# V1 and V0 as 32 by 64 matmuls over row groups, with their operand loaded by DMA, and the bias constant's matmuls in a later step

## The chip, the cores and the metric

The kernel runs on one core of one Trainium2 chip. Time is device time in microseconds of that core, the median of several executions. The engines are named as the profile names them: PE is TensorE (PEld its weight loads), DVE is VectorE, ACT is ScalarE, POOL is GpSimd, and SP is SyncE, which only issues DMAs here. Each engine runs its own instructions in program order and waits on semaphores for the others.

## The reference

A compressed interaction network (CIN) over x of shape (1024, 64, 16): batch, F = 64 features, E = 16. Three layers; the first two keep half of their outputs as the next h, and only sums over E of the outputs reach the result, through one row of weights.

```python
for i in range(3):
    z = jnp.einsum('bfe,bge->bfge', x0, h).reshape(Bn, f0 * fh, e)
    y = jnp.einsum('oc,bce->boe', Ws[i], z) + bs[i][None, :, None]
    if i != 2:
        x_i, h = y[:, :64, :], y[:, 64:, :]
    else:
        x_i, h = y, y
    xs.append(x_i)
pooled = jnp.sum(jnp.concatenate(xs, axis=1), axis=2)
return pooled @ fc_w.T + fc_b
```

All arithmetic is in f32.

## The kernel before, in words

Because the result is one number for each batch row, the kernel never forms the outputs that only get summed. It folds the final weights into the layers: the last layer becomes a 64-column matrix Q (called w_all[:, :, 64:128]), the summed halves of layers 1 and 0 become the 64 by 64 matrices V1 (v1w) and V0 (held twice on the diagonal of bd). For each column (b, e) the result is then a sum over h1 times (Q's matmul plus V1 x), and x times (V0 x plus a constant cx).

The batch is cut into NCH = 32 chunks of 32 rows, so a chunk is N = 512 columns. A chunk's data comes in two layouts from HBM: `xa` (128 rows, 4 shifted copies, 1 MB) and `xb` (the same size), by `load_xa` and `load_xb` on SP's queue. DVE multiplies them in `product` (L212), four products j of 128 by 2048; ACT writes squares into 32 rows of the last one (L217). PE contracts the 16 tiles of a chunk with `w_all` in `contract` (L249), sixteen f32 matmuls of 128 by 128 by 512. The profile records each f32 matmul twice, as two passes.

The diagonal that the products leave out, V1 and V0 are done for four chunks at once in `contract_shared`, called with the first of them; the text calls one such call a group, and there are eight. It has three parts. L263 multiplies V1, 64 by 64, with x of a chunk: even chunks have x in rows 0 to 63 of `xxs[k]` (k = chunk // 2), odd ones in rows 64 to 127; the result goes to the other half of the chunk's accumulator. L267 multiplies V0 with the same x into `ys[k]`. L273 multiplies the squares of x (`sqs`, four chunks on four row groups of 32) with `w_sq`, as 32 by 64 tiles, eight for a group. Before the change `last_tile` makes these operands on ACT, a chunk at a time: `squares` (L223, 32 rows) and a copy into `xxs` (L232, 64 rows).

The order of work is written out by hand; no planner moves instructions. The head chunks [2, 3, 0, 1] are computed first for h1 alone, in `half_contract` (L285), while the weights Q are made from W2 and W1 (L409, L433, a round trip through DRAM `md`, and L534). PE's first work is a row of matmuls on zeros (L105), then the shift matmuls (L182) that make the second operand of the first products on chip. Early on PE also computes the bias constant `cst` (L366: fc times biases, four records, read by ACT at L370 and used at L613 when results are finished). The head's chunks 0 and 1 get their Q part at once (`head_q`, L303), chunks 2 and 3 after chunk 7.

The main loop goes over `order` = [4, 5, 6, 7, 2, 3, 8, 9, ...]. In step s it emits the loads and products of the chunk two places on (`load_products`), the contraction of chunk order[s], the group where chunk % 4 is 1 (for chunks 0 to 3, in the step of chunk 3), and `factors`, `x_v0x` and `sums` of finished chunks: ACT copies half of an accumulator (q, L319), DVE multiplies it by the other half (uu, L325), multiplies x by V0 x (L330) and sums over e (L334). V1 and V0 are made on DVE on the way, by `weigh` (L571, L572) and four copies each (L583 after chunk 4's products, L595 after chunk 5's).

Buffers set when transfers start: `xa` and `xb` have three each, products twelve (three chunks), accumulators four banks. SP issues in order, so a load that waits for a buffer holds up what is behind it.

Of the kernel before, what the change touches and what calls it, by code (L numbers as in the profile page):

```python
# [33 lines left out]
F32 = mybir.dt.float32  # L37
AF = mybir.ActivationFunctionType
# [3 lines left out]
F = 64  # L42
E = 16
B = 1024
CB = 32
N = CB * E
# [5 lines left out]
XR = 128 + NI  # L52
EXT = 96
HEAD = [2, 3, 0, 1]
NF = len(HEAD)
KEPT = HEAD[-2:]
NV = 200
FIRST = 4
# [4 lines left out]
def cin_kernel(ctx, tc, xra, xrb, wh, w0r, w1h, w2t, wx1, wx0, vec, out):  # L63
    nc = tc.nc
# [10 lines left out]
    def const_tile(name, shape):  # L75
        return const.tile(shape, F32, tag=name, name=name)
# [18 lines left out]
    fv2 = const_tile("fv2", [128, 32])  # L95
    nc.scalar.copy(fv2, fc2.to_broadcast([128, 32]))

    bd = const_tile("bd", [128, 128])

    misc = ps.tile([128, N], F32, tag="acc", name="misc", bufs=4)  # L100


    zeros = nc.const_aps.tensor(0.0, [128, 128])
    for n in (128,) * 7 + (64,):
        nc.tensor.matmul(misc[:, 0:n], zeros, zeros[:, 0:n], start=True, stop=True)  # L105

    shift = const_tile("shift", [128, 96])
# [13 lines left out]

    w_all = const_tile("w_all", [128, NT, 192])
    w_sq = const_tile("w_sq", [128, 192])
    v1w = const_tile("v1w", [128, F])


    xas, xbs, xxs, sqs = {}, {}, {}, {}

    def load_xa(c, at=slice(0, NI)):
        if c not in xas or at.start == 0:  # L130
# [9 lines left out]
    def load_xb(c, first=NJ):  # L140

        xb = xp.tile([128, NJ, N], F32, tag="xb", name=f"xb_{c}")
        for at in (slice(0, first), slice(first, NJ)):
            if at.start < NJ:
                nc.sync.dma_start(out=xb[:, at, :], in_=xrb[c, :, at, :])
        xbs[c] = [xb[:, j, :] for j in range(NJ)]

    def load_chunk(c):
        load_xa(c)
# [2 lines left out]
    c0, c1, c2, c3 = HEAD  # L152
# [63 lines left out]
        if j == NJ - 1:  # L216
            nc.scalar.activation(zs[c, j][SQ, 0, :], xas[c][SQ, 0, :], AF.Square)  # L217

    def squares(c):
        if c // 4 not in sqs:  # L220
            sqs[c // 4] = xp.tile([128, N], F32, tag="zl", name=f"sq_{c}", bufs=3)
        at = slice(32 * (c % 4), 32 * (c % 4) + 32)
        nc.scalar.activation(sqs[c // 4][at], xas[c][0:32, 0, :], AF.Square)  # L223

    def last_tile(c):

        if c >= FIRST:
            squares(c)
        if c % 2 == 0:
            xxs[c // 2] = sp.tile([128, N], F32, tag="xx", name=f"xx_{c}", bufs=5)  # L230
        to = halves[c % 2]
        nc.scalar.copy(xxs[c // 2][to], xas[c][to, 0, :])  # L232

    def w_cols(c):
        return slice(64, 192) if c % 2 else slice(0, 128)

    def tiles(j):

        return (1, 2, 3, 0) if j == NJ - 1 else range(NI)
# [14 lines left out]
    def contract_shared(first):  # L254

        chunks = range(first, first + 4)
        ends = chunks if first == 0 else chunks[:2]
        for k in (first // 2, first // 2 + 1):
            ys[k] = ps.tile([128, N], F32, tag="y", name=f"y_{k}")
            for n in range(2):  # L260
                c, rows, q = 2 * k + n, halves[n], halves[1 - n]
                for acc_c, cols in pieces(c):
                    nc.tensor.matmul(  # L263
                        acc_c[q], v1w[rows], xxs[k][rows, cols], start=(c not in ends), stop=False,
                    )
            for rows in halves:
                nc.tensor.matmul(ys[k][rows], bd[rows, rows], xxs[k][rows], start=True, stop=True)  # L267
        for c in chunks:
            at = slice(32 * (c % 4), 32 * (c % 4) + 32)
            for acc_c, cols in pieces(c):  # L270
                for n in range(2):
                    h = n == c % 2
                    nc.tensor.matmul(  # L273
                        acc_c[halves[n]], w_sq[at, w_cols(c)][:, 64 * n : 64 * n + 64],
                        sqs[first // 4][at, cols], start=h and (first == 0 or c not in ends),
                        stop=(c in ends), tile_position=(at.start, 64 * n),
                    )


    def half_contract(c, *js, last=None, at=None):  # L280
        for j in js:
            for i in at or tiles(j):
                t = j * NI + i
                for n in range(2):
                    nc.tensor.matmul(  # L285
                        accs[c][halves[n]], w_all[:, t, 0:64],
                        zs[c, j][:, i, n * H2 : (n + 1) * H2],
                        start=(t == 0), stop=(j == last and i == tiles(j)[-1]),
                    )
# [56 lines left out]


    new_acc(c0, H2)
    squares(c0)
    nc.scalar.copy(xb_gps[:, 0, :], xbs[c0][1])  # L350
    xbs[c0][1] = xb_gps[:, 0, :]
    for i in (0, 2):
# [6 lines left out]
    nc.scalar.copy(w0o[0], w0s[0][:, :, 1, :])  # L359
    h1_weights(0, w0o[0])  # L360
    product(c0, 0, 2, NI)
    half_contract(c0, 0, at=(0, 1))

    cst = const_tile("cst", [128, 1])
    for j in range(2):
        nc.tensor.matmul(  # L366
            misc[:, 0:1], fcol[:, j : j + 1].to_broadcast([128, 128]), bcol[:, j : j + 1],
            start=(j == 0), stop=(j == 1),
        )
    nc.scalar.activation(cst, misc[:, 0:1], AF.Identity, bias=fcb, scale=float(E))  # L370
    nc.scalar.copy(w0o[1], w0s[1][:, :, 1, :])
    product(c0, 2, 0, 2)
    h1_weights(1, w0o[1])
# [3 lines left out]
    nc.vector.memset(w0o[3][SQ, 0, :], 0.0)  # L377
    for j in (2, 3):
        h1_weights(j, w0o[j])
    half_contract(c0, 0, at=(2, 3))  # L380


    for j, tag in ((0, "y"), (3, "acc"), (1, "y"), (2, "set")):
# [4 lines left out]
    new_acc(c1, H2)  # L388
    nc.scalar.copy(xb_gps[:, 1, :], xbs[c1][3])
    xbs[c1][3] = xb_gps[:, 1, :]  # L390
    squares(c1)

    product(c0, 3)
    load_chunk(c3)
# [7 lines left out]


    v2r = flat_tile("v2r")[:, 0:1024].rearrange("p (n c) -> p n c", n=2)
    v2t = const_tile("v2t", [128, F])
    for n in range(2):
        pv = ps.tile([128, 512], F32, tag=("set", "y")[n], name=f"pv2_{n}")
        for k in range(4):
# [68 lines left out]
    keep_h1(c1)  # L477


    squares(c2)  # L480
    new_acc(c2, H2)
    for j in range(NJ):
        product(c2, j)
# [34 lines left out]
    new_acc(c3, H2)  # L518
    for j in range(NJ - 1):
        product(c3, j)  # L520
    squares(c3)
    keep_h1(c2)
    half_contract(c3, 0, 3, 1, 2, last=2)

    for j in range(1, NJ):
        for half in range(2):
            read_columns(j, nc.scalar if half and j == 2 else nc.sync, half)
    dg = const_tile("dg", [128, F])
    nc.sync.dma_start(out=dg[SQ], in_=m_ap(32, 32, [[row + F, 32], [1, F]]))
    nc.sync.dma_start(out=w_sq[:, 64:128], in_=m_ap(0, 0, [[0, 4], [row + F, 32], [1, F]]))  # L530

# [2 lines left out]
        nc.vector.tensor_tensor(w_all[:, at, 64:128], ms[:, 0, at], ms[:, 1, at], ALU.add)  # L534

    keep_h1(c3)
    for c in KEPT:
        last_tile(c)


    for j in range(NJ):
# [10 lines left out]
    for j in range(NJ):  # L552
        head_q(0, j)

    made = set()

    def load_products(c, other=None):

        for n in (c,) if other is None else (c, other):
            if n not in made:  # L560
                load_chunk(n)
                last_tile(n)
                made.add(n)
        for j in range(NJ):
            product(c, j)

    def weigh(w, fc, out):
# [3 lines left out]
        nc.vector.tensor_tensor(w, w, fc.unsqueeze(1).to_broadcast([128, nk, n]), ALU.mult)  # L571
        nc.vector.tensor_reduce(out, w, AX.X, ALU.add)  # L572

    load_products(FIRST)


    w1x = set_tile("w1x")
    nc.sync.dma_start(out=w1x, in_=wx1)
    v1h = const_tile("v1h", [128, 32])
    weigh(w1x, fcr[:, 64:128], v1h)  # L580
    for to in halves:
        for n in range(2):
            nc.vector.tensor_copy(v1w[to, 32 * n : 32 * n + 32], v1h[halves[n]])  # L583

    load_products(FIRST + 1)

    def v0_weights():
        w0x = flat_tile("w0x")
        nc.sync.dma_start(out=w0x, in_=wx0)
        v0h = const_tile("v0h", [128, 32])  # L590
        weigh(w0x, fcr[:, 0:64], v0h)
        for to in halves:
            for n in range(2):
                cols = slice(to.start + 32 * n, to.start + 32 * n + 32)
                nc.vector.tensor_copy(bd[to, cols], v0h[halves[n]])  # L595


    NP = NCH // 2
    QP = NP // 4
    res = const_tile("res", [128, QP, CB])  # L600
    outs = out.rearrange("(k h b) o -> h k (b o)", h=2, b=CB)

    def pool(k0, k1, part=0, **flags):
# [16 lines left out]
    for s, c in enumerate(order):  # L620
        k, head = c // 2, c in HEAD
        if order[s - 1] in HEAD and not head:
            for n in range(NF // 2):
                x_v0x(n)
            for n in HEAD:
                factors(n)
                if n % 2:
                    sums(n // 2)
        if 0 < s < len(order) - 2 and s not in (2, 3):
            load_products(*order[s + 2 : s + (4 if s == 6 else 3)])  # L630
        if s in (2, 3):

            if s == 2:
                for n in order[4:6]:
                    load_chunk(n)
                    last_tile(n)
            for j in (0, 1) if s == 2 else (2, 3):
                for n in order[4:6]:
                    product(n, j)
        if not head:  # L640
            if c % 4 < 2:
                new_acc(c)
            for j in range(NJ):
                contract(c, j)
        elif c % 2:
            for n in (c - 1, c):
                new_acc(n)
            for j in range(NJ):
                head_q(k, j)
            contract_shared(0)  # L650
        if c % 4 == 1 and not head:
            for n in (1, 2):
                new_acc(c + n)
            contract_shared(c - 1)
        if s == 0:
            v0_weights()
            load_products(order[2], order[3])

        if c == HEAD[0] or c % 4 in (0, 3) and s and order[s - 1] not in HEAD:
            factors(order[s - 1])  # L660
            if order[s - 1] % 2:
                sums(order[s - 1] // 2)
        elif c % 4 == 2 and not head:
            factors(c - 2)
            factors(c - 1)
            x_v0x(k - 1)
            x_v0x(k)
            sums(k - 1)
# [94 lines left out]
```

## Time and profile before

| | us |
|---|---|
| median of 6 runs | 486.85 |
| lowest and highest | 486.42, 487.24 |
| profiled execution | 486.5 |
| its span (first to last instruction) | 484.7 |
| PE busy | 479.1 |
| DVE busy | 370.3 |
| ACT busy | 94.4 |
| a group of L263, L267 and L273 (83.92 to 86.84) | 2.92 |
| granted TensorE clock, mean | 0.998 |
| DMA, mean over the span | 162 GB/s |

Lines of the profile name the line of the kernel, the engine, the operation, its tiles as out<-in and their shapes. "busy" is the union of the instructions' times, so parallel matmuls count once. The chain of work that ended last follows the end of the program back through whatever released each step; a line of it is start, length, engine, tile, line and number of records. A timeline line is start, length, engine, line, operation and number of records merged in it.

### The profile page before, as it was taken

The numbers are of one execution on the slowest core, as the hardware profiler recorded it, in microseconds if no ns is written. First come the engines' busy times: TensorE is split into PE (matmuls) and PEld (weight loads), VectorE is DVE, ScalarE is ACT, GpSimd is POOL, SyncE is SP. The second block draws the span as 40 slices with busy tenths as digits, with TensorE's granted clock in tenths as the row PEclk, the third lists the DMA queues.
The fourth block names the chain that finished last, engine by engine and source line by source line (L and its number), as shares of the span: only waits on it lengthen the run. The fifth ranks groups of instructions, "written<-read, shape, count | busy, mean of one in ns | idle before, by whom it ended". The sixth has DMA issues, their size and how long they took to land.

```text
span 484.7 us, 4065 instructions
## 1 busy us (share of the span) xinstructions
PE 479.1 (99%) x1674; PEld 215.6 (44%) x1674; DVE 370.3 (76%) x235; ACT 94.4 (19%) x166; POOL 15.2 (3%) x15
## 2 busy tenths in 40 slices
PE   8999999999999999999999999999999999999996
PEld 5565344443344344444444344443444434444465
DVE  5993699999899989898887686767878676771312
ACT  4254012021213030322221012212022121020001
POOL 5330000000000000000000000000000000000000
PEclk9999999999999999999999999999999999999999
DMA  8985984441743453546253344432244430000000
GB/s 340 412 259 165 423 370 174 172 174 42 319 171 163 173 191 156 185 172 272 106 216 124 141 174 173 162 133 107 118 173 173 174 144 29 1 0 0 1 1 0
DMA packets 14392, 78.59 MB, mean 162 GB/s; under 512 B 3778, under 2 KB 4450, under 8 KB 5478
## 3 DMA queue, kind: packets, MB, share of 16 engines
q1 hardware_dynamic: 13314, 77.31, 40.9%
q10 hardware_dynamic: 1060, 1.02, 0.8%
q8 instruction: 13, 0.21, 0.2%
q14 instruction: 5, 0.04, 0.0%
HBM read 76.69 MB, written 1.64 MB: 162 GB/s over the span
## 4 chain that ended last, share of the span: by engine, by line
PE 98%; DMA 1%; DVE 0%; ACT 0%; SPq 0%; issue 0%
PE acc L249 80%; PE acc L285 6%; PE acc L303 6%; PE acc L263 3%; PE acc L273 2%; DMA w0t<-in_wh 1%; PE xp L182 0%; PE pm L433 0%; PE pv L409 0%; PE y L267 0%; SPq L132 0%; PE po L605 0%; PE misc L366 0%; DVE uu L325 0%; DVE w_all L342 0%
## 5 line engine op out<-in xcount | busy, mean ns | idle before, releaser
L249 PE MATMUL acc<-z,w_all 128*128 128x512 f32 (+1 forms) x928 | 387.3, 579 | 0.0
L212 DVE TENSOR_TENSOR z<-xa,xb 128x2048 f32<-128x2048 f32 x124 | 278.4, 2286 | 40.8 <-PE acc L249 34.1
L249 PEld LDWEIGHTS acc<-z,w_all 128*128 128x128 f32 x928 | 175.5, 190 | 211.3 <-issue 205.7
L217 ACT ACTIVATE z<-xa 32x512 f32<-32x512 f32 x34 | 21.3, 626 | 318.4 <-DVE z L212 317.1
L325 DVE SCALAR_TENSOR_TENSOR uu<-acc,vs,q 64x512 f32<-64x512 f32 (+1 forms) x29 | 21.2, 732 | 57.7 <-ACT q L319 57.5
L285 PE MATMUL acc<-z,w_all 128*64 128x256 f32 x256 | 29.0, 381 | 0.9 <-DVE w_all L342 0.9
L303 PE MATMUL acc<-z,w_all 128*64 128x512 f32 x128 | 27.9, 593 | 0.0
L319 ACT COPY q<-acc 64x512 f32<-64x512 f32 (+1 forms) x33 | 18.7, 567 | 37.4 <-PE acc L249 21.2
L212 DVE TENSOR_TENSOR z<-xa,xp 128x2048 f32<-128x2048 f32 (+2 forms) x12 | 20.4, 1748 | 5.9 <-PE xp L182 5.9
L285 PEld LDWEIGHTS acc<-z,w_all 128*64 128x64 f32 x256 | 17.9, 137 | 12.7 <-issue 2.5
L223 ACT ACTIVATE sq<-xa 32x512 f32<-32x512 f32 x32 | 20.1, 628 | 8.4 <-issue 4.1
L334 DVE TENSOR_REDUCE acc<-uu 128x64 f32<-128x1024 f32 (+3 forms) x19 | 20.3, 1072 | 0.3
L232 ACT COPY xx<-xa 64x512 f32<-64x512 f32 x32 | 19.6, 613 | 0.3
L303 PEld LDWEIGHTS acc<-z,w_all 128*64 128x64 f32 x128 | 9.1, 137 | 18.0 <-issue 17.6
L267 PE MATMUL y<-xx,bd 64*64 64x512 f32 x64 | 15.5, 603 | 0.0
L263 PE MATMUL acc<-xx,v1w 64*64 64x512 f32 (+1 forms) x66 | 15.5, 588 | 0.0
L330 DVE SCALAR_TENSOR_TENSOR uu<-y,cx,xx 128x512 f32<-128x512 f32 x16 | 11.3, 746 | 0.2
L212 POOL TENSOR_TENSOR z<-xa,xb_gps 128x1024 f32<-128x1024 f32 (+1 forms) x3 | 9.3, 3102 | 5.1 <-ACT xb_gps L350 4.4
L273 PE MATMUL acc<-sq,w_sq 32*64 32x512 f32 (+1 forms) x132 | 8.9, 599 | 0.0
L263 PEld LDWEIGHTS acc<-xx,v1w 64*64 64x64 f32 x66 | 4.1, 132 | 10.6 <-issue 10.5
L534 DVE TENSOR_TENSOR w_all<-ms 128x256 f32<-128x256 f32 x4 | 1.5, 422 | 6.0 <-DMA ms<-md 6.0
L212 POOL TENSOR_TENSOR z<-xa,xb 128x2048 f32<-128x2048 f32 x1 | 4.6, 4567 | 12.9 <-DMA xb<-in_xrb 12.9
(57 smaller groups left out, 63.6 us busy)
## 6 DMA issues: line engine op xcount, KB each, us to landing
xa<-in_xra SPq DMA_DIRECT2D x32, 1024.0 KB, 4.8
xb<-in_xrb SPq DMA_DIRECT2D x31, 1024.0 KB, 6.9
w<-in_w2t SPq DMA_DIRECT2D x2, 1024.0 KB, 10.9
xa<-in_xra SPq DMA_DIRECT2D x2, 768.0 KB, 7.9
w1s<-in_w1h SPq DMA_DIRECT2D x1, 1024.0 KB
w1x<-in_wx SPq DMA_DIRECT2D x1, 1024.0 KB
w0x<-in_wx SPq DMA_DIRECT2D x1, 1024.0 KB, 9.1
w0t<-in_w0r SPq DMA_DIRECT2D x1, 768.0 KB
```

What stands on the lines that cost most here:

```text
L212: engine.tensor_tensor(zs[c, j][:, at, :], xas[c][:, at, :], xbs[c][j].unsqueeze(1).to_broadcast([128, last - first, N]), ALU.mult,)
L217: nc.scalar.activation(zs[c, j][SQ, 0, :], xas[c][SQ, 0, :], AF.Square)
L223: nc.scalar.activation(sqs[c // 4][at], xas[c][0:32, 0, :], AF.Square)
L232: nc.scalar.copy(xxs[c // 2][to], xas[c][to, 0, :])
L249: nc.tensor.matmul(acc_c, w_all[:, t, w_cols(c)], zs[c, j][:, i, cols], start=(t == 0 and c % 4 < 2), stop=(t == NT - NI and c % 4 >= 2),)
L263: nc.tensor.matmul(acc_c[q], v1w[rows], xxs[k][rows, cols], start=(c not in ends), stop=False,)
L273: nc.tensor.matmul(acc_c[halves[n]], w_sq[at, w_cols(c)][:, 64 * n : 64 * n + 64], sqs[first // 4][at, cols], start=h and (first == 0 or c ...
L285: nc.tensor.matmul(accs[c][halves[n]], w_all[:, t, 0:64], zs[c, j][:, i, n * H2 : (n + 1) * H2], start=(t == 0), stop=(j == last and i == ...
L303: nc.tensor.matmul(accs[c][halves[1 - c % 2]], w_all[:, t, 64:128], zs[c, j][:, i, :], start=(t == 0), stop=False,)
L319: nc.scalar.copy(q[h, cols], acc_c[64 - h.start : 128 - h.start])
L325: nc.vector.scalar_tensor_tensor(uu[:, cols], acc_c[h], bh1[h], q[h, cols], ALU.add, ALU.mult)
L334: nc.vector.tensor_reduce(acc[rows, of, k, half], uus[k][rows, of, E * half.start : E * half.stop].rearrange("p k (b e) -> p k b e", e=E), ...
```

## The change

Four things change.

- `load_shared(first)` takes the place of `squares` and `last_tile`. For the four chunks of a group it loads `xr`, a tile of 128 rows by 2 by 512, by one DMA for each chunk: row group n (32 rows) holds chunk first + n, features 0 to 31 in part 0 and 32 to 63 in part 1. Another DMA for each chunk loads `xxs`, which DVE still reads in `x_v0x`. One ACT instruction squares part 0 for all four chunks. It is called where the chunk 4k+1 is loaded, and for chunks 0 to 3 in step 2.
- In `contract_shared` V1 and V0 become 32 by 64 matmuls, two (m = 0, 1) for each chunk and matrix, accumulated over the two halves of the features. The tile positions put chunk c on rows 32 (c % 4) and the two matrices on the two column halves. Weights are `v1w` and `v0w`, each on all four row groups, filled by `to_groups`, 16 ACT copies of 32 by 32 each, in place of the DVE copies.
- The bias constant's matmuls move from the start to step 9 (before the contraction of chunk 11), with a PSUM tile of their own. The contraction of chunk 2's first product, which they split in two, is emitted in one piece.
- One zero matmul of 128 columns fewer at the start (seven in place of eight), and some tiles share storage (v2t, dg and res; shift, v1h and v0h).

```diff
-    for n in (128,) * 7 + (64,):
+    for n in (128,) * 6 + (64,):
         nc.tensor.matmul(misc[:, 0:n], zeros, zeros[:, 0:n], start=True, stop=True)
...
+    def load_shared(first):
+
+        xr = xrs[first] = sp.tile([128, 2, N], F32, tag="xr", name=f"xr_{first}")
+        for k in (first // 2, first // 2 + 1):
+            xxs[k] = sp.tile([128, N], F32, tag="xx", name=f"xx_{k}", bufs=4)
+        for n in range(4):
+            c = first + n
+            nc.sync.dma_start(
+                out=xr[32 * n : 32 * n + 32],
+                in_=bass.AP(
+                    tensor=xra.tensor, offset=c * XR * N, ap=[[N, 32], [32 * N, 2], [1, N]]
+                ),
+            )
+            nc.sync.dma_start(out=xxs[c // 2][halves[c % 2]], in_=xra[c, 0:F])
+        sqs[first] = sp.tile([128, N], F32, tag="sq", name=f"sq_{first}")
+        nc.scalar.activation(sqs[first], xr[:, 0, :], AF.Square)
...
-            for n in range(2):
-                c, rows, q = 2 * k + n, halves[n], halves[1 - n]
+        groups = {c: slice(32 * (c % 4), 32 * (c % 4) + 32) for c in chunks}
+        for m in range(2):
+            for c, at in groups.items():
+                n, xr = c % 2, xrs[first][groups[c], m]
                 for acc_c, cols in pieces(c):
                     nc.tensor.matmul(
-                        acc_c[q], v1w[rows], xxs[k][rows, cols], start=(c not in ends), stop=False,
+                        acc_c[halves[1 - n]], v1w[at, m], xr[:, cols],
+                        start=(m == 0 and c not in ends), stop=False,
+                        tile_position=(at.start, 64 * (1 - n)),
                     )
-            for rows in halves:
-                nc.tensor.matmul(ys[k][rows], bd[rows, rows], xxs[k][rows], start=True, stop=True)
+                nc.tensor.matmul(
+                    ys[c // 2][halves[n]], v0w[at, m], xr, start=(m == 0), stop=(m == 1),
+                    tile_position=(at.start, 64 * n),
+                )
...
-    half_contract(c0, 0, at=(0, 1))
-
-    cst = const_tile("cst", [128, 1])
-    for j in range(2):
-        nc.tensor.matmul(
-            misc[:, 0:1], fcol[:, j : j + 1].to_broadcast([128, 128]), bcol[:, j : j + 1],
-            start=(j == 0), stop=(j == 1),
-        )
-    nc.scalar.activation(cst, misc[:, 0:1], AF.Identity, bias=fcb, scale=float(E))
...
-    half_contract(c0, 0, at=(2, 3))
+    half_contract(c0, 0)
...
-                last_tile(n)
+                if n % 4 == 1:
+                    load_shared(n - 1)
...
+    def to_groups(w, part):
+
+        for at in range(0, 128, 32):
+            for n in range(2):
+                for m in range(2):
+                    q = 64 * n + 32 * m
+                    nc.scalar.copy(
+                        w[at : at + 32, m, 32 * n : 32 * n + 32], part[q : q + 32]
+                    )
...
-    for to in halves:
-        for n in range(2):
-            nc.vector.tensor_copy(v1w[to, 32 * n : 32 * n + 32], v1h[halves[n]])
+    to_groups(v1w, v1h)
...
-        for to in halves:
-            for n in range(2):
-                cols = slice(to.start + 32 * n, to.start + 32 * n + 32)
-                nc.vector.tensor_copy(bd[to, cols], v0h[halves[n]])
+        to_groups(v0w, v0h)
...
+        if s == len(HEAD) + 5:
+
+            pc = ps.tile([128, 1], F32, tag="set", name="pc")
+            for j in range(2):
+                nc.tensor.matmul(
+                    pc, fcol[:, j : j + 1].to_broadcast([128, 128]), bcol[:, j : j + 1],
+                    start=(j == 0), stop=(j == 1),
+                )
+            nc.scalar.activation(cst, pc, AF.Identity, bias=fcb, scale=float(E))
```

## The prediction

> **What bounds the kernel now.** I read the busy shares first, then the chain of work that ended last, then that chain in order of time, then TensorE's timeline in the stretches that the edit touches. All times are of the profiled execution: 486.5 us, of which 484.7 are span and 1.8 lie around it. The median of the six runs, 486.85, is 0.35 above it.
>
> ```profile
> PE 479.1 (99%) x1674; PEld 215.6 (44%) x1674; DVE 370.3 (76%) x235; ACT 94.4 (19%) x166; POOL 15.2 (3%) x15
> ...
> PE 98%; DMA 1%; DVE 0%; ACT 0%; SPq 0%; issue 0%
> ```
>
> PE is busy for 99% of the span and carries 98% of the chain; DVE, at 76%, is next and has room. So only what shortens or stalls PE's stream counts. The chain in order of time, around a group of shared matmuls:
>
> ```profile
> 7.63 1.08 PE acc L285 x8
> 8.71 0.54 PE misc L366 x4
> 9.25 1.01 PE acc L285 x8
> ...
> 83.99 0.58 PE acc L263 x2
> 84.58 0.42 PE acc L263 x2
> 85.01 0.42 PE acc L263 x2
> 85.44 0.42 PE acc L263 x2
> 85.86 1.04 PE acc L273 x16
> 86.91 27.66 PE acc L249 x64
> ```
>
> From 7.63 to 480.57 us, where the tail of about 4 us begins, every piece is PE without a wait. An f32 matmul is two records ("passes"): 64 full ones take 27.66 us, 0.43 each. A group costs 1.87 us for V1 and V0 and 1.04 for the squares. PE's timeline of the same group shows why (start, then duration):
>
> ```profile
> 82.97 1.02 PE L249 MATMUL acc<-z,w_all 128*128 128x512 f32 x2
> 83.92 0.65 PE L263 MATMUL acc<-xx,v1w 64*64 64x512 f32 x2
> 83.93 0.65 PE L267 MATMUL y<-xx,bd 64*64 64x512 f32 x2
> 84.40 0.60 PE L263 MATMUL acc<-xx,v1w 64*64 64x512 f32 x2
> 84.41 0.60 PE L267 MATMUL y<-xx,bd 64*64 64x512 f32 x2
> 84.83 0.60 PE L263 MATMUL acc<-xx,v1w 64*64 64x512 f32 x2
> 84.84 0.60 PE L267 MATMUL y<-xx,bd 64*64 64x512 f32 x2
> 85.26 0.60 PE L263 MATMUL acc<-xx,v1w 64*64 64x512 f32 x2
> 85.27 0.59 PE L267 MATMUL y<-xx,bd 64*64 64x512 f32 x2
> ...
> 86.28 0.63 PE L273 MATMUL acc<-sq,w_sq 32*64 32x512 f32 x8
> 86.84 0.70 PE L249 MATMUL acc<-z,w_all 128*128 128x512 f32 x1
> ```
>
> Four 64 by 64 tiles start together, so a pass of four costs the 0.43 of one; eight 32 by 64 tiles do so too (the squares: eight second passes at 86.28). The steps between starts are 0.48, 0.43, 0.43, then 0.54 from 85.26 to the squares' first at 85.80 (the timeline has it a line on), 0.48 to 86.28, 0.56 to the next full matmul. The change of shape at 85.80 thus costs 0.11 over a plain step, and the first step after a change 0.05 more.
>
> **The change, part by part.**
>
> *The groups (V1, V0, squares), eight times.* Before: 4 passes of four 64 by 64 tiles, then 2 of eight 32 by 64 tiles. After: 2 + 2 + 2 passes of eight 32 by 64 tiles. Still six steps of 0.43, and the matmuls rise from 16 to 24, but the shape changes once less: 0.11 + 0.05 = 0.16 saved. The bill that stays (entry, first step, exit) I take from the rows above. Ends: the chain gives 1.04 - 0.86 = 0.18 at most; on the other side nothing in the trace shows V1 and V0 on 32 rows, and if two of the eight had to take turns, a step pair of 0.86 comes in. I take 0.16, since the nearest row, the squares, has the same eight tiles, the same two per row group that read the same rows of SBUF, and the same four row groups behind one column half. Eight groups: **-1.28 us**. The last group, with chunk 31 in two pieces, takes 449.24 to 452.21 = 2.97 against 2.92; I leave it at the same gain.
> The Trainium skill, "TensorEngine Tiling (Array Packing)", Restrictions and Gotchas, Gotcha 1, speaks against this: different row tiles, it says, cannot access the same PSUM bank at the same time. The new V0 matmuls of chunks 4k and 4k+1 do just that in one y bank. But so do the two L267 tiles before, rows 0 to 63 and 64 to 127 into the two halves of one y tile, and they start together (84.41, x2). By the rule each half of V0 would need a pair of passes more, 2 x 0.86 x 8 = 13.7 us, and the sum would be about 499; I go by the row.
>
> *The bias constant.* Its four L366 records leave the start and come back in step 9, after chunk 10. At the start PE gains from 9.18 (the second L285 batch) back to the end of the product it needs: DVE's L212 from 7.49 takes 1.21 and ends at 8.70, plus 0.05 for the semaphore (weights done at 7.57, first L285 at 7.63). So PE resumes at 8.76 and gains **-0.42** (ends: 0 if a later DVE step absorbs it, -0.54, the chain's piece). I looked for such a step. PE reaches the next L285 at 10.8 (POOL's first product is ready at 9.0, its second at 11.36 against a need of 11.6), L433 at 24.5 (its weights come at 22.9), L303's second quarter at 45.6 (its weights at 45.1), chunk 4 at 55.9 (first product at 54.6). All have cover, the thinnest 0.3 us. ACT's 2.2 us wait for this constant goes too, but DVE, not ACT, sets the next weights there (busy from 7.15 on), so that is worth nothing.
> Later the four records cost PE their steps. From 8.64 to 9.18 is 0.54 with two changes of shape; inside a stream of full matmuls there are none, and the loads start 0.11 apart: 4 x 0.11 = **+0.44** (ends 0.34, the four-pass pool step at 476.57 in the chain, and 0.63). The instruction on ACT now waits there for PE; behind it stands the q copy of chunk 10, some 0.3 to 0.7 us later, and behind that DVE's uu. DVE's products run two chunks (27 us) ahead, which covers it.
>
> *Fewer zeros.* One full set and so two passes of 0.21 go. The shift matmuls, which follow them at 4.36, start up to 0.42 sooner, and DVE's first products with them. DVE then waits at 7.15 all the same, for ACT's copy (6.75 to 7.13) of w0t, which lands at 6.72. **0**. Ends: -0.02, and for the other side the clock: the first shift pass takes 0.88 (4.36 to 5.24), the following 0.43, so the clock rises inside this stretch, after 4.4 us of PE work. PE then idles 0.93 us to 7.63, and would idle 1.35 after. If that lost the clock until a like 4.4 us had passed, up to 2.2 us. I take 0: the gap stays short beside the time that it took to rise.
>
> *Weights v1w and v0w.* Eight DVE copies (0.74 + 0.76 us) become 32 small ACT copies. ACT steps for such are 0.26 apart (L421, two in 0.51) or 0.15 (L547): 16 take 2.4 to 4.2 us. v0h is ready at 80.0 - 0.78 = 79.2, the copies end at 81.6 to 83.4, PE wants them at 83.92 - 0.42 = 83.50. **0**, with 0.1 us of cover at the worst end; without it PE waits some 0.3 us, once. ACT has nothing due in that stretch (idle 78.69 to 89.76). v1w has 14 us.
>
> *Loads by row groups.* Per group 8 DMAs of 128 KB on SP's queue, placed after chunk 4k+1's xa and xb, replace ACT work (four squares of 0.63 and four copies of 0.61 us become one square of about 0.63). Behind them on SP stands chunk 4k+2; at 0.33 to 0.45 us an issue it is issued up to 3.6 us later, plus about 1 MB, 2.5 us at the 425 GB/s of the full stretch 48 to 70 us. The first group meets that stretch: w0x (DVE wants it at 74.7; 10 MB from 45.1 on are through by about 70) and chunks 6 and 7 move 2.5 us and still land 7 us or more early. Later DMA is at 35 to 42% and loads lead by two chunks. ACT's new wait for xr stands ahead of the square of chunk 4k+1's last product: xr of the first group lands near 62, that product ends near 75. **0**.
>
> Sum: -1.28 - 0.42 + 0.44 = **-1.26 us**: 485.2 for the profiled execution, 486.85 - 1.26 = **485.6** for the median. 0.2% (0.97 us) is about what a measurement of this kernel can tell from no change.
>
> **The rivals.**
> 1. *Row groups take turns* (slower). Two of the eight matmuls, V1 and V0 of different row groups, can't run at once, and each group gets one step pair more: 8 x 0.86 = 6.9, so 492.4. Against it: the squares' eight at 86.28, L267's pair. For it: no row with 32-row tiles accumulating two halves into one y bank. It decides from 0.28 us per group on (1.26 + 0.97 over 8). Chance 0.10, with 0.05 more for another stall of over 2.2 us (the clock, or a late xr in each group).
> 2. *The start's gain is swallowed, the constant costs its upper end*: -1.28 + 0 + 0.63 = -0.65, 486.2. For it: covers of 0.3 us at 11.4 and 0.1 at 83.4. Chance 0.16.
> 3. *The group saves nothing*: 24 matmuls instead of 16 cost in weight loads or waits between them what the shape change did. -1.26 + 1.28: 486.9, no change. Against it: eight loads and eight matmuls start 7 ns apart in the squares. Chance 0.09.
>
> **How the numbers follow.** The forecast has 0.60, all of it faster by over 0.2%, though 485.6 lies just 0.3 us beyond that bound. Rivals 2 and 3 give 0.25 for no change, rival 1 and the like 0.15 for slower. The forecast's own range, from the ends of its terms (-0.18 x 8 - 0.54 + 0.34, and -0.16 x 8 - 0.30 + 0.60), is 485.2 to 485.9; to hold 8 in 10 it must take in rivals 2 and 3 and the scatter of the runs (0.4 us to either side): **484.8 to 487.1**.
>
> **What would show it.** Right: in the group, eight starts together, steps of 0.43 from V1's second pass to the last squares with no 0.54 among them, 2.75 us from first start to next full matmul (2.92 before); L285's second batch near 8.76; the constant's four records near PE's 11th chunk with 0.44 between full matmuls; no PE wait near 83.5. Wrong: a start of V0 a pass after V1's, a PE wait on ACT at the first group or on DVE between 9 and 56 us, or passes of 0.43 where 0.21 stand after 7.63.

## The result and the profile after

The changed kernel takes 485.32 us (median of 18 runs, 485.01 to 485.73); the kernel before 486.82 on the same chips. The ratio is 0.9968, with a 95% interval of 0.9959 to 0.9977: faster by 0.32%, or 1.5 us. The profiled execution took 485.47 us, 483.7 of it span (before: 486.5 and 484.7).

The head of the page of the changed kernel, busy times and the engines' shares of the chain that ended last:

```profile
PE 478.4 (99%) x1802; PEld 217.5 (45%) x1802; DVE 368.7 (76%) x227; ACT 67.2 (14%) x142; POOL 15.3 (3%) x15
...
PE 98%; DVE 1%; issue 0%; ACT 0%
```

PE still carries 98% of the chain, with 128 records more than before. ACT gave up 27 us of work; groups64 below shows that nothing came of that by itself. The chain in order of time (start, length, what, records):

```profile
6.05 0.63 DVE z L232
...
7.25 0.41 DVE w_all L352
7.67 1.14 DVE z L232
...
8.85 1.08 PE acc L295 x8
...
83.66 0.57 PE acc L270
...
85.57 0.86 PE acc L283 x16
86.42 27.66 PE acc L254 x64
...
161.16 13.93 PE acc L254 x32
175.09 0.34 PE pc L646 x4
175.43 41.31 PE acc L254 x96
```

Three things are to be seen. The squares (L283, before L273) take 0.86 in place of 1.04: they no longer pay for a change of shape. The bias constant's four records stand at 175.09. And the chain now passes through DVE at 6.05 to 8.81, where before it passed through the landing of w0t. In the kernel before the same chain had:

```profile
1.68 5.04 DMA w0t<-in_wh
...
7.15 0.43 DVE w_all L342
```

TensorE's timeline of the first group after (start, duration):

```profile
83.59 0.64 PE L270 MATMUL acc<-xr,v1w 32*64 32x512 f32 x1
83.60 0.64 PE L275 MATMUL y<-xr,v0w 32*64 32x512 f32 x1
83.61 0.64 PE L270 MATMUL acc<-xr,v1w 32*64 32x512 f32 x1
83.61 0.64 PE L275 MATMUL y<-xr,v0w 32*64 32x512 f32 x1
...
83.64 0.64 PE L275 MATMUL y<-xr,v0w 32*64 32x512 f32 x1
84.07 0.59 PE L270 MATMUL acc<-xr,v1w 32*64 32x512 f32 x1
...
84.50 0.59 PE L270 MATMUL acc<-xr,v1w 32*64 32x512 f32 x1
...
84.93 0.59 PE L270 MATMUL acc<-xr,v1w 32*64 32x512 f32 x1
...
85.36 1.06 PE L283 MATMUL acc<-sq,w_sq 32*64 32x512 f32 x16
86.35 0.70 PE L254 MATMUL acc<-z,w_all 128*128 128x512 f32 x1
```

Eight matmuls start within 0.05 us, and the steps are 0.48, 0.43, 0.43, 0.43 with no 0.54 among them. From first start to the next full matmul it is 2.76 us, against 2.92.

To compare executions I use a length below that I call the stream: from PE's first half_contract matmul to the end of its last full one. It is 472.9 us before (7.63 to 480.56) and 471.8 after (7.72 to 479.54): 1.1 us shorter. What lies ahead of the stream differs from execution to execution: over all profiles below it starts between 7.37 and 8.05 us. So the stream shows what the change did to PE's work, and a median also carries the scatter of the start.

### The profile page after: what moved, and what is told of

Same layout as the page of the kernel before. It is cut to its first block, busy times and chain, and to the rows that moved or that the text cites. A ratio compares the mean times of both kernels' runs of the same rounds, so it can differ in the third digit from the quotient of the medians.

```text
span 483.7 us, 4409 instructions
## 1 busy us (share of the span) xinstructions
PE 478.4 (99%) x1802; PEld 217.5 (45%) x1802; DVE 368.7 (76%) x227; ACT 67.2 (14%) x142; POOL 15.3 (3%) x15
## 3 DMA queue, kind: packets, MB, share of 16 engines
q10 hardware_dynamic: 1060, 1.02, 0.8%
## 4 chain that ended last, share of the span: by engine, by line
PE 98%; DVE 1%; issue 0%; ACT 0%
PE acc L254 80%; PE acc L313 6%; PE acc L295 6%; PE acc L270 3%; PE acc L283 1%; PE xp L202 1%; PE misc L107 1%; PE pm L432 0%; PE pv L408 0%; DVE z L232 0%; PE y L275 0%; PE po L607 0%; DVE uu L335 0%; DVE acc L344 0%; DVE w_all L352 0%
## 5 line engine op out<-in xcount | busy, mean ns | idle before, releaser
L275 PE MATMUL y<-xr,v0w 32*64 32x512 f32 x128 | 15.9, 600 | 0.0
L270 PE MATMUL acc<-xr,v1w 32*64 32x512 f32 (+1 forms) x132 | 15.7, 587 | 0.0
L270 PEld LDWEIGHTS acc<-xr,v1w 32*64 32x64 f32 x132 | 5.1, 131 | 9.9 <-issue 9.6
L283 PE MATMUL acc<-sq,w_sq 32*64 32x512 f32 (+1 forms) x132 | 8.7, 574 | 0.0
L166 ACT ACTIVATE sq<-xr 128x512 f32<-128x512 f32 x8 | 5.0, 630 | 3.2 <-DMA xr<-in_xra 3.0
L202 PE MATMUL xp<-xa,shift 64*64 64x512 f32 x32 | 5.4, 780 | 0.0
L283 PEld LDWEIGHTS acc<-sq,w_sq 32*64 32x64 f32 x132 | 3.4, 132 | 3.8 <-issue 3.5
```

The costliest lines, as they stand in the source:

```text
L270: nc.tensor.matmul(acc_c[halves[1 - n]], v1w[at, m], xr[:, cols], start=(m == 0 and c not in ends), stop=False, tile_position=(at.start, 6 ...
L275: nc.tensor.matmul(ys[c // 2][halves[n]], v0w[at, m], xr, start=(m == 0), stop=(m == 1), tile_position=(at.start, 64 * n),)
L283: nc.tensor.matmul(acc_c[halves[n]], w_sq[at, w_cols(c)][:, 64 * n : 64 * n + 64], sqs[first][at, cols], start=h and (first == 0 or c not ...
```

## The experiments

**groups64: the old matmul shapes in the changed kernel.**

```diff
-        for m in range(2):
-            for c, at in groups.items():
-                n, xr = c % 2, xrs[first][groups[c], m]
...
+        for k in (first // 2, first // 2 + 1):
+            for n in range(2):
+                c, rows, q = 2 * k + n, halves[n], halves[1 - n]
...
+                        acc_c[q], v1w[rows], xxs[k][rows, cols], start=(c not in ends), stop=False,
...
+                nc.tensor.matmul(ys[k][rows], bd[rows, rows], xxs[k][rows], start=True, stop=True)
```

> The changed kernel with V1 and V0 back as 64 by 64 matmuls on xxs (weights by DVE copies, as before); loads, constant and zeros stay as changed. Theory (the gain is the change of shape that a group no longer makes): a group takes 2.92 us again in place of 2.76, the gain of the groups (7 of 0.16, the last of 0.01 in the trace) goes, 485.3 + 1.1 = 486.4 us. Rival (the gain comes from the operands, which ACT no longer makes, 27 us of its work): nothing changes but the group's own length, the time stays at 485.3.

486.54 us, ratio to the kernel before 0.9994 (0.9985 to 1.0002). The chain in order of time around its first group:

```profile
83.79 0.58 PE acc L270 x2
...
85.67 1.04 PE acc L279 x16
```

Seven groups take 2.92 again and the last 2.97, the squares 1.04, the stream 473.0. Without the new shapes the gain is gone as far as the timing can tell, although the eight loads and ACT's smaller work are still there. The rival falls.

**shape_again: one change of shape more in the kernel before.**

```diff
+        def squared():
+            for c in chunks:
...
         for k in (first // 2, first // 2 + 1):
...
-        for c in chunks:
...
+            if k == first // 2:
+                squared()
```

> The kernel before, with all squares' matmuls of a group moved between its two halves of V1 and V0: same matmuls, one change of shape more (64, 32, 64 rows). Theory: 0.16 us more for each of eight groups, 2.92 becomes 3.08, 486.8 + 1.3 = 488.1 us. Rival (what the changed kernel saved is not the shape change but the second V step or the accumulators' waits): under 0.05 a group, 486.8 to 487.2.

487.72 us, ratio 1.0022 (1.0013 to 1.0031). The chain in order of time around its first group:

```profile
84.04 0.58 PE acc L277 x2
...
85.06 1.04 PE acc L265 x16
86.10 0.58 PE acc L277 x2
...
87.12 3.20 PE acc L249 x7
```

The second half of V1 and V0, which took 0.85 in the kernel before, begins with 0.58 again. Seven groups are 3.08 us, as expected; the last, with its pieces, 3.10 in place of 2.97. The stream is 474.2, 1.24 longer, as the theory has it. The median rose by less, 0.96 over the 486.76 of the kernel before in the same round, and fell 0.4 short of the 488.1; that part lies ahead of the stream and is not explained. A change of shape thus costs 0.16 us in a group of this kernel, added or removed.

**zeros8: the eighth set of zeros back.**

```diff
-    for n in (128,) * 6 + (64,):
+    for n in (128,) * 7 + (64,):
```

> The changed kernel with the eighth set of zeros back. Theory (the clock rises after a fixed stretch of PE work, so fewer zeros put more of the shift matmuls on the slow clock): the shift matmuls start near 4.4 us and only their first step takes 0.88, DVE's first product starts near 5.9 in place of 6.05, PE's first L295 0.1 sooner, 485.2 us. Rival (the clock plays no part): the first product starts 0.2 to 0.4 later than in the changed kernel, PE's first L295 0.1 or more later, 485.4 or more.

485.46 us, 0.9972 (0.9961 to 0.9983). This profile had the shift matmuls fast from the first step on, DVE's first product at 5.49 and the stream from 7.37: better than either theory said, and cst_idle shows the same fast steps with seven sets, so it is no effect of the zeros. The stream is 471.8 to the digit. The median is 0.14 above the changed kernel's, which the scatter covers.

The clock is read here off the steps of the shift matmuls: 0.43 us for four at the full clock, 0.85 to 0.88 where it is slow. The granted clock in the profile's rows does not show this: it reads 1.00 from 4.9 to 6.6 us of the changed kernel, where the steps take 0.85. So wherever the text says that the clock rose, that is inferred from steps that halve.

**cst_idle: the bias constant in PE's idle stretch at the start.**

```diff
     shift_pair(c0, (2, 3))
+    for j in range(2):
+        nc.tensor.matmul(
+            misc[:, 0:1], fcol[:, j : j + 1].to_broadcast([128, 128]), bcol[:, j : j + 1],
+            start=(j == 0), stop=(j == 1),
+        )
...
     nc.scalar.copy(w0o[0], w0s[0][:, :, 1, :])
+    cst = const_tile("cst", [128, 1])
+    nc.scalar.activation(cst, misc[:, 0:1], AF.Identity, bias=fcb, scale=float(E))
```

> The changed kernel with the bias constant's matmuls ahead of the first half_contract, where PE idles (0.93 us in the kernel before), ACT's instruction after its first copy of w0t. Theory (four records cost 0.45 in the stream of full matmuls and nothing in the idle stretch): 485.3 - 0.45 = 484.9 us, step 9 without the gap of 0.45. Rival (they push back the first L295, or the zeros' bank): PE's first L295 0.3 to 0.5 later than in the changed kernel, time the same, 485.3.

485.02 us, 0.9964 (0.9951 to 0.9978). The chain at step 9:

```profile
160.94 55.13 PE acc L259 x128
```

The stream is 471.37: the 0.45 is gone from step 9 (in the changed kernel the same stretch, 161.16 to 216.74, took 55.58), and the first half_contract starts at 7.51, after PE has idled 0.95 us. The price of the four records where the change put them is shown; that they are free in the idle stretch too.

**best: the same, with the eighth set of zeros and V0 ahead of V1.**

```diff
+                nc.tensor.matmul(
+                    ys[c // 2][halves[n]], v0w[at, m], xr, start=(m == 0), stop=(m == 1),
+                    tile_position=(at.start, 64 * n),
+                )
                 for acc_c, cols in pieces(c):
...
-                nc.tensor.matmul(
-                    ys[c // 2][halves[n]], v0w[at, m], xr, start=(m == 0), stop=(m == 1),
-                    tile_position=(at.start, 64 * n),
-                )
```

> The changed kernel with three edits: the bias constant's matmuls in PE's idle stretch at the start, the eighth set of zeros back, and in a group each chunk's V0 matmul ahead of its V1 matmuls. Theory: the four records' 0.45 go; in the last group (2.96 in place of 2.76, since the two 256-column pieces of chunk 31's V1 stand ahead of its V0) V0 no longer starts late, 0.1 to 0.2; 485.3 - 0.6 = 484.7 us. Rival (the last group is long because of the pieces themselves, not their order): it stays at 2.96 and the time is 484.9.

484.84 us, 0.9962 (0.9949 to 0.9974). The last group fell from 2.96 to 2.78, so it was the order, since cst_idle and zeros8, which have the other two edits one by one, keep 2.96. In the changed kernel the two 256-column pieces of chunk 31's V1 stand ahead of its V0, and the last V0 pass starts 0.21 after its neighbour (TensorE's timeline of the changed kernel):

```profile
449.60 0.59 PE L275 MATMUL y<-xr,v0w 32*64 32x512 f32 x1
...
449.81 0.59 PE L275 MATMUL y<-xr,v0w 32*64 32x512 f32 x1
```

The stream is 471.34, not the 471.2 of the sum. The chain shows where PE waited, and the timelines of ACT and DVE show for what:

```profile
11.29 0.09 issue
11.37 1.95 PE acc L300 x16
```

```profile
10.39 0.38 ACT L378 COPY w0p<-w0t 128x256 f32<-128x256 f32 x1 [2.29 <-DMA w0t<-in_w0r]
10.80 0.42 DVE L357 TENSOR_TENSOR w_all<-w0t,w0p 128x256 f32<-128x256 f32 x1 [0.55 <-ACT w0p L378]
```

PE waits at 11.29, and the batch starts 1.17 us after the shift matmuls ahead of it (10.20 to 11.37) and not 1.02, as it does in the changed kernel. What is late is not POOL's product, whose first half was ready at 9.53 and whose second, at 11.85, is wanted for the second half of the batch, at about 12.3. It is the batch's weights: DVE's w_all ends at 11.22, because it waited for ACT's copy, and ACT for the landing of the second part of w0t at 10.39. In the changed kernel that copy starts at 9.21, in best2 at 9.12. The prediction's list of covers has POOL's products there and not these weights.

**best2: the same with seven sets of zeros.**

> The changed kernel with the bias constant's matmuls in PE's idle stretch at the start and V0 ahead of V1 in a group; zeros as changed (seven sets), which lets POOL start up to 0.4 sooner than with eight. Theory: the stream is 471.8 - 0.45 - 0.18 = 471.2, 0.15 shorter than with the eighth set of zeros, where the half_contract of j = 1 waited for POOL; 484.7 us. Rival (the zeros play no part in that wait): 471.35 and 484.85.

485.08 us, 0.9968 (0.9956 to 0.9981). Stream 471.2, as the theory had it. But the wait that the expectation puts down to POOL was the one for w0t's second part, which landed in time here, and no run shows that the zeros have a part in that. In time neither best nor best2 can be told from the changed kernel; by their streams they are 0.5 and 0.6 us shorter.

**zeros0: nearly no zeros.**

```diff
-    for n in (128,) * 6 + (64,):
+    for n in (64,):
```

> The changed kernel with all zeros but one of 64 columns taken away. Theory (the clock rises only after some 4 us of PE work): the shift matmuls start near 3.7 us, all four steps take 0.88, and the first half_contract runs at 0.43 a pass for a while, so PE's stream starts 0 to 0.5 later and loses 0.5 to 1: 485.8 to 486.8 us. Rival (zeros only hold up the shift matmuls): steps of 0.43 after the first, DVE's first product at 5.3 or sooner, 485.3 or less.

485.51 us, 0.9974 (0.9965 to 0.9983). Theory and rival both miss. The shift matmuls start at 3.91 when their data lands, and their steps are slow throughout, as the theory said. But the half_contract from 7.61 on runs at full speed and the stream is 471.8: nothing was lost. So the clock was up by 7.6 us with 4.1 us of PE work behind it and an idle stretch of 2.5 us in between. The median is 0.2 above the changed kernel's: leaving out nearly all zeros cannot be told from leaving out one set.

**act_made: operands made by ACT in place of the loads.**

```diff
-                if n % 4 == 1:
-                    load_shared(n - 1)
+                last_tile(n)
...
+        for m in range(2):
+            nc.scalar.copy(xrs[first][at, m], xas[c][32 * m : 32 * m + 32, 0, :])
+        nc.scalar.activation(sqs[first][at], xas[c][0:32, 0, :], AF.Square)
+        nc.scalar.copy(xxs[c // 2][halves[c % 2]], xas[c][halves[c % 2], 0, :])
```

> The changed kernel with the operands of all groups but that of chunks 0 to 3 made by ACT from xa (two copies of 32 rows, a square of 32 and a copy of 64 for each chunk) in place of the eight loads. Theory (loads against ACT work is worth nothing, since PE sets the end and both are covered): ACT busy 67 us becomes some 130, DMA bytes fall, groups stay at 2.76, 485.3 +- 0.2 us. Rival (the loads, or the ACT work that they spare, carry a part of the gain of 1.5 us, of which the lengths of PE's stretches show 1.1): 485.7 or more.

487.2 us, 1.0011 (1.0002 to 1.0019): slower than either kernel. My theory falls. The time is where the rival put it (485.7 or more), though not because the groups had gained by the loads. Seven groups are as in the changed kernel; the first takes 4.30 us in place of 2.76, 1.5 of the 1.9 us between the medians. ACT's timeline ahead of it:

```profile
78.31 3.65 ACT L590 COPY v0w<-shift 32x32 f32<-32x32 f32 x16 [3.90 <-DVE shift L582]
81.98 1.26 ACT L178 COPY xr<-xa 32x512 f32<-32x512 f32 x2
83.25 0.63 ACT L179 ACTIVATE sq<-xa 32x512 f32<-32x512 f32 x1
...
84.53 1.26 ACT L178 COPY xr<-xa 32x512 f32<-32x512 f32 x2
85.82 0.63 ACT L179 ACTIVATE sq<-xa 32x512 f32<-32x512 f32 x1
```

The operands of chunks 6 and 7 stand behind the 16 copies of v0w, which wait for DVE; PE is due at 83.6; the first half of chunk 7's xr is there at about 85.2, the second at 85.8, its squares at 86.5. In the kernel before they were made at 76.2 to 78.7, while DVE made the weights. So putting the weight copies on ACT is affordable in this order of work because the operands left ACT. (This variant has two ACT copies more for each chunk than the kernel before, so 1.5 us is the price of the variant.)

**shared_first: the first eight loads ahead of chunk 4.**

```diff
+                if n == FIRST:
+                    load_shared(n)
                 load_chunk(n)
-                if n % 4 == 1:
+                if n % 4 == 1 and n != FIRST + 1:
```

> The changed kernel with the eight shared loads of chunks 4 to 7 ahead of chunk 4's xa and xb on SP's queue in place of behind chunk 5's. Theory (the loads cost nothing only because they stand behind what PE needs next): chunk 4's first product, 1.3 us ahead of PE in the kernel before, comes 2.5 to 8 us later, PE idles 1.2 to 7 us before the first L254, 486.5 to 492 us. Rival (the first loads have cover anywhere): 485.3.

491.65 us, 1.0089 (1.0061 to 1.0118). The chain in order of time:

```profile
50.39 8.09 DMA xb<-in_xrb
58.60 2.30 DVE z L232
61.04 29.33 PE acc L254 x64
```

Chunk 4's contraction starts at 61.04, not 56.00, and its 64 passes with chunk 5's take 29.33, not 27.66: 6.7 us in this execution; the medians are 6.3 apart, and the six runs scatter from 487.83 to 493.11. The same eight loads that cost nothing behind chunk 5 cost this in front of chunk 4.

**before_again and after_again: both kernels once more.** They are line for line the kernels before and after.

> The kernel before, line for line. What is open: medians differ by 1.5 us, PE's stream from its first L285 (its first half_contract) to its last full matmul by 1.1. Theory (executions scatter in the start, by the clock's rise and the landing of w0t, and a median of a few runs carries 0.2 to 0.4 of that): within 0.3 of 486.8 either way, and the first L285 of this profile off from 7.63 by up to 0.4. Rival (each built kernel has a fixed offset of its own in the start): below 486.6 here, with the stream at 472.9 all the same.

> The changed kernel, line for line, with the same question. Theory: 485.3 +- 0.3, stream 471.8, first L285 anywhere from 7.3 to 8.1. Rival (a fixed offset): 485.5 to 485.8, which is 486.8 less the 1.1 of the stream.

486.78 (0.9996, 0.9978 to 1.0015) and 485.36 us (0.9975, 0.9966 to 0.9985). The medians come back within 0.05 us, and the rival of the changed kernel falls (485.5 to 485.8). That of the kernel before is not as clear: the kernel before itself, run 20 times in the same round, gave 486.47, which is 0.3 below this copy of it and below the rival's 486.6. Against that number the changed kernel is 1.1 us faster, which is the stream and no more. The profiles show how the start can differ. First the kernel before, in this second profile (the chain in order of time), then TensorE's timeline of its shift matmuls, and of those of zeros8, which also start at 4.36:

```profile
0.78 3.64 PE misc L106 x16
4.43 1.93 PE xp L183 x8
...
6.38 0.51 DVE z L213
...
8.05 1.08 PE acc L286 x7
```

```profile
4.36 3.16 PE L183 MATMUL xp<-xa,shift 64*64 64x512 f32 x16
```

```profile
4.36 1.95 PE L202 MATMUL xp<-xa,shift 64*64 64x512 f32 x16
```

The same 16 records from the same moment take 3.16 us in one execution and 1.95 in another. Where the clock rises late, the chain runs through the zeros and the shift to DVE's first product (6.38), and the stream starts at 8.05; where it rises early, through the landing of w0t, and it starts at 7.37 to 7.68 with eight sets. In the changed kernel, late rises give 7.72 and 7.62. The landing of w0t scatters as well: in groups64, with seven sets and an early rise, it holds the stream back to 7.85.

```profile
0.78 3.22 PE misc L108 x14
4.00 1.93 PE xp L203 x8
...
5.95 0.60 DVE z L233
```

That is after_again: the same chain as before_again with two zero passes, 0.42 us, fewer. Between these two profiles, both with a late rise, the dropped zeros are worth 0.4 us; where the chain runs through w0t they are worth nothing.

## Why the prediction was right, and where it was not

The forecast was 485.6, its own range 485.2 to 485.9; 485.32 was measured. By its terms:

| term | predicted | measured, and where |
|---|---|---|
| seven groups | 7 x -0.16 | 7 x -0.16 (2.92 to 2.76); groups64, shape_again |
| last group | -0.16 | -0.01 (2.97 to 2.96); best |
| constant away from the start | -0.42 | -0.42 (first to second batch: 7.63 to 9.18, now 7.72 to 8.85) |
| constant in step 9 | +0.44 | +0.45 (cst_idle) |
| fewer zeros | 0 | 0 or -0.4 by the profile; by the medians of zeros8 and zeros0 not told from 0 |
| weights, loads | 0 | 0 |
| stream | -1.26 | -1.11 |

*The groups* went as argued, for the reason argued. The Trainium skill's rule on PSUM banks ("TensorEngine Tiling (Array Packing)", Restrictions and Gotchas), weighed there, is not what this trace shows: the L275 matmuls of chunks 4 and 5, on two row groups and into the two halves of one y bank, start at 83.60 and 83.61. Rival 1 had no part, and rivals 2 and 3 fall with the first and third lines of the table: the start's gain came, and so did the groups'.

*The last group* was the first mis-sized term. "I leave it at the same gain" was wrong: two short pieces ahead of V0 on the same rows held it back by up to 0.2 us, and 0.15 of the 0.16 went there.

*The constant* was a move at no gain, as the sum had it: it left a place where it cost 0.42 for one where it costs 0.45. What the working missed is that the place for it was one line up in the trace: PE idled 0.93 us at 6.70.

*Fewer zeros* was argued from a bound that did not hold: "DVE then waits at 7.15 all the same, for ACT's copy". That was read from one execution, with an early rise. In the changed kernel's profile, with a late one, ACT's copy ended at 7.04 and DVE, busy with its own products, came to the weights at 7.25. The prediction also took the clock to rise "after 4.4 us of PE work"; in shape_again it was up by 4.03, after some 3.3 us, and in the changed kernel, busy from 0.78, not yet at 6.6. What the term is worth stays open. With the last group's loss the stream is 1.1 us shorter and not 1.26, yet the medians differ by 1.5. The remaining 0.4 lies ahead of the stream. That the zeros are its cause is not shown, and two runs speak against all of it being theirs: with the eighth set back zeros8 takes 485.46, with nearly none zeros0 takes 485.51, both within 0.2 of the changed kernel. The kernel before itself moved between 486.47 and 486.82 from round to round, which is nearly as much. The two intervals (0.9959 to 0.9977, 0.9966 to 0.9985) have 1.1 to 1.7 us in common. So the stream fell 0.15 us short of the forecast, which the last group explains, and the median went 0.3 beyond it, which no run explains.

*The range.* The upper end of the forecast's own range was added up with -0.30 and +0.60, where the ends that the terms name are 0 and +0.63; with those it is 486.2 and not 485.9. The result lies in both.

*The weights* had cover: ACT's 16 copies of v0w took 3.67 us (0.23 each) and ended at 82.48, PE came at 83.59. *The loads* cost nothing, but one step of that was badly wrong. SP's timeline in the changed kernel:

```profile
47.17 0.46 SPq L158 DMA_DIRECT2D xr<-in_xra  x1
...
51.92 0.32 SPq L158 DMA_DIRECT2D xr<-in_xra  x1
...
60.38 0.47 SPq L164 DMA_DIRECT2D xx<-in_xra  x1
60.95 0.53 SPq L594 DMA_DIRECT2D w0x<-in_wx  x1
```

The eight issues took 13.8 us, not 3.6: SP waited for earlier loads to land before it issued the next (from 46 to 62 us its waits for xa, xb and w1x add up to 9.8 us; why it has to wait is not shown). w0x was issued at 60.95, 8 us later than before. It was still in time, since DVE wants it at 74; shared_first shows what such a delay costs where the cover is 1.3 us.

## What to carry to other kernels

Count the changes of a matmul's tile shape as work: here each costs 0.16 us on a PE that never idles, and regrouping to one shape paid although it needed half as many matmuls again. Small matmuls whose result is needed late belong into a stretch where PE idles, not into any later step: four records were free in the idle stretch at the start and cost 0.45 us in the stream. And read a start-up from more than one profile before calling a term there zero: the chain can run through another engine in the next execution.

## What the runs showed that I had not expected

- The moment at which PE's clock rises, as the steps show it, differs between executions of one kernel. The kernel before had only its first shift step slow in one profile (2.34 us for the 16 records) and more of them in the other (3.16). The shift matmuls were fast from the first step at 4.07 us in cst_idle, and still slow in a step from 5.77 to 6.6 in the changed kernel, though PE had been busy from 0.78 on in both; with nearly no zeros (zeros0) the clock was up by 7.6 us. The Trainium skill ("TensorE: Matmul & The Clock Gate", Part 1) says that the window that decides is free-running and does not start with the kernel. The traces are consistent with that, though they don't show the window itself, and the spread in them is over 2 us.
- A queue of small loads behind large ones is issued at the pace at which the large ones land (13.8 us for eight issues of 0.3 to 0.6 us in the first such group).
- With two tiles of 256 columns on one row group, the matmul behind them on the other column half starts late, although it uses another tile (by 0.21 us at 449.81; best against the changed kernel, 0.18 us in one group).
